# A two-layer spectral metaformer block: filter and weight set-up inside the ramp's ticks, and a finer order of the full tick

## The chip, the cores and the metric

One core of a Trainium2 chip runs the whole program. The metric is the device time of one execution in microseconds. The kernel before takes 5155.03 (median of 3 runs, 5151.31 to 5158.59).

A core has a matrix engine (TensorE, PE in the rows; PEld is its weight loading), VectorE (DVE), ScalarE (ACT), GpSimd (POOL) and SyncE (SP), which in this kernel issues all the transfers. Each works through its own list in order and waits on the others through semaphores.

## The reference

The input is 8 images of 128 x 128 pixels with 96 channels. Two layers follow each other, and each has two residual halves: a spectral convolution, and a small feed-forward net on every pixel. What one layer computes, cut to its core:

```python
z = (x - mean(x)) / sqrt(var(x) + 1e-6)                  # per pixel, over 96 channels
a = scale * relu(z @ w1.T)**2 + bias                     # 96 -> 192
F = rfft2(a)                                             # per channel, 128 x 65
r = softmax(soa(concat(mean(z), mean(relu(bn(z @ sp_w.T)))) @ fc1.T) @ fc2.T)
filt = [Rh @ cw @ Rw.T for cw in (cw0, cw1, cw2)]        # 16x9, 8x4, 24x13 -> 128 x 65
x = x + irfft2(F * sum(r[s] * filt[s])) @ w2.T           # 192 -> 96
z = (x - mean(x)) / sqrt(var(x) + 1e-5)
h = relu(q16(q8(z) @ q8(W1) + q8(b1)))                   # 96 -> 384; q8 is float8e5, q16 float16
x = x + q16(q8(h) @ q8(W2) + q8(b2))                     # 384 -> 96
```

The three filters of a layer are given small and are resized by two fixed matrices, Rh and Rw, before use. The filters do not depend on the image; the three weights r do.

## The kernel before

**Stages and groups.** Two layers of 8 images make 16 jobs, and each job is cut into 16 groups of 8 rows (or, in the middle stage, of 4 frequencies), so every stage has 256 groups. There are three stages, each a generator that yields between its steps:

- P (`pixels`): load x (step 0), statistics, scale on POOL (line 507), transpose on PE (`pt_a`), evict with ScalarE (`xT`), project in two halves (`pw0`, `pw1`, line 522), relu and square on ScalarE (`r`, `xs`), sum and difference of row pairs (`sd`, line 540), transform along the width (`pa0`, `pa1`, line 549), and store to memory (`a_d`, line 569).
- F (`frequencies`): load a_d and the half-resized filter `u_d` (tiles `al`, `ut`), weigh the filter on POOL (line 656), resize it along the height on PE (`pf`, line 668), transform along the height (`py`, line 702), multiply on VectorE (`pr`), add on POOL (`xf`), project to 96 channels (`pz`, lines 776 and 784), transform back (`pi`), and store (`y_d`). One group of 16 is "packed": it holds the two real frequencies, with an extra product `px`.
- S (`tokens`): load y_d and x, transform back along the width (`ps_r`), add, statistics and normalisation (`xn_c`), transpose (`pt_c`), and the feed-forward net in three blocks (`pm0` to `pm2`, evicted as `y16`, then `a16` and a cast to float8 `h`), second product (`po`), eviction (`o16`), bias (line 905), final addition on POOL and store (line 908).

N is the shared normalisation arithmetic of a tick; G is an image's gate (the softmax r).

**Ticks.** The program is a loop over ticks t from -4 to 299. F runs 19 groups behind P and S 40 behind. In each tick a written list gives the order of the steps: an entry ("S", 21, -2) gives step 21 of S to the group two behind. There are five lists: RAMP (t below 15, P alone), RISE (t = 15 to 37, P and F), TICK (t = 38 to 257, all three), FALL (258 to 275, F and S) and TAIL (S alone). The order of issue on each engine is the order of the list, since the kernel is written under a manual schedule:

```python
for place, (stage, step, ahead) in enumerate(order):
    for gate_step, image in gates.get(place, ()):
        advance("G", gate_step, image)
    i = t - offset[stage] + ahead
    advance(stage, step, i if stage == "N" else min(i, n - 1))
```

**Banks.** PSUM is cut into four double banks. `BANKS` (one table for each list) says which of the four a tile uses. A group of matmuls can start when the last reader of the tile before it in that bank is done, so a list and its bank table together decide where TensorE waits.

**Set-up.** Before the loop, `prepare` loads and prepares the weights of both layers, `load_filters` loads their filters, and `small_filters` resizes them along the width: for each layer 12 blocks of four products (line 284, 8 matmul instructions), two copies on ScalarE (298), two on VectorE (296), and a store to `u_d` (300). All of it stands ahead of the first x load in every engine's list, SP's included. Line numbers are those of the kernel before.

Of the kernel before, what the change touches and what calls it, by code (L numbers as in the profile page):

```python
# [10 lines left out]
F32 = mybir.dt.float32  # L11
F16 = mybir.dt.float16
# [28 lines left out]
UN = 8  # L41
NA, NY = 3, 3
LAG = 3
WE = M + SC
# [3 lines left out]
NORM_ACT, NORM_ACT_TAIL = (4, 5, 6, 7), (0, 1, 3, 4, 5, 7)  # L48
CAST_ACT, CAST_ACT_TAIL = (0, 1, 2), ()
SD_POOL_RAMP = ((0, 1), (1, 1))  # L50
# [3 lines left out]
    ("S", 4, 0), ("S", 21, -2), ("P", 10, -1), ("P", 11, -1), ("P", 0, 4), ("F", 2, 1),  # L54
    ("F", 3, 1), ("P", 2, 1), ("P", 1, 2), ("S", 5, 0), ("F", 4, 1), ("P", 12, -1),
    ("S", 6, 0), ("S", 22, -2), ("S", 1, 1), ("F", 5, 1), ("S", 7, 0), ("S", 14, -1),
    ("S", 2, 1), ("F", 9, 0), ("P", 3, 1), ("S", 8, 0), ("P", 13, -1), ("S", 15, -1),
    ("P", 14, -1), ("S", 16, -1), ("N", 0, 0), ("S", 17, -1), ("P", 4, 1), ("S", 9, 0),
    ("F", 6, 1), ("P", 5, 0), ("N", 1, 0), ("F", 10, 0), ("P", 15, -1), ("F", 11, 0),
    ("P", 6, 0), ("N", 2, 0), ("F", 7, 1), ("P", 16, -1), ("P", 17, -1), ("P", 18, -1),  # L60
    ("S", 10, 0), ("F", 12, 0), ("S", 0, 3), ("P", 19, -1), ("F", 13, 0), ("S", 11, 0),
    ("S", 18, -1), ("P", 7, 0), ("F", 8, 1), ("F", 14, 0), ("S", 12, 0), ("P", 8, 0),
    ("F", 0, 3), ("F", 1, 2), ("F", 15, 0), ("S", 19, -1), ("S", 13, 0), ("S", 3, 1),
    ("S", 20, -1), ("P", 9, 0),
# [3 lines left out]
    1: ((26, 0), (44, 1), (52, 2), (53, 3), (55, 4), (59, 5), (61, 6)),  # L68
    2: ((23, 7), (35, 8), (41, 9), (48, 10)),
# [3 lines left out]
    ("P", 1, 2), ("F", 3, 1), ("N", 0, 0), ("F", 4, 1), ("P", 3, 1), ("P", 5, 0),  # L73
    ("F", 10, 0), ("P", 14, -1), ("P", 15, -1), ("P", 0, 3), ("P", 4, 1), ("P", 6, 0),
    ("F", 5, 1), ("F", 11, 0), ("N", 1, 0), ("P", 16, -1), ("P", 17, -1), ("P", 7, 0),
    ("P", 8, 0), ("F", 6, 1), ("F", 7, 1), ("F", 1, 2), ("P", 18, -1), ("P", 19, -1),
    ("F", 12, 0), ("F", 8, 1), ("P", 9, 0), ("N", 2, 0), ("P", 10, 0), ("P", 2, 2),
    ("P", 11, 0), ("F", 13, 0), ("F", 14, 0), ("F", 0, 3), ("P", 12, 0), ("F", 2, 2),
    ("F", 15, 0), ("P", 13, 0), ("F", 9, 1),
)  # L80

# [924 lines left out]
```

## Time and profile before

| what | us |
|---|---|
| median of 3 runs | 5155.03 |
| the profiled execution, and its span | 5158.86, 5156.8 |
| first load of x issued | 109.75 |
| POOL scaling (L507) of the 1st, 4th and 18th group starts | 118.5, 138.1, 234.1 |
| its pace: ramp, rise, full ticks | 6.9, 14.3, 18.6 (most) |
| final addition (L908) in the fall and the tail, pace | 14.1, 8.8 |
| POOL idle until the bias (L905) before L908 | 1032.4 in 220 waits |
| mean granted TensorE clock | 0.983 |

The profile is of one execution. A row of instructions gives start and duration in us, then engine, line, operation, the tile written and the tiles read, the shape and a count; in brackets the idle time of the engine before it and what ended it. A row of a group gives a total in us, the mean of one in ns, and the idle time before. A row by stretch gives the busy time of each engine in a window with the number of its instructions. In a chain where every group starts as the last one lets it, the difference of two starts is what the first group costs; its own duration is some 0.2 longer, since matmuls overlap at their ends.

### The profile page before, as it was taken

The page shows a single profiled execution, that of the slowest core. Times are in us where ns is not written, and L with a number is a line of the kernel's source. Part 1 is how long each engine was busy: PE and PEld are TensorE (multiplying, and loading weights), DVE is VectorE, ACT ScalarE, POOL GpSimd, SP SyncE. Part 2 cuts the span into 40 slices and gives each one's busy share as a digit, 9 for nine tenths or more (in the row PEclk, how much of TensorE's full clock was granted, in tenths as well). Part 3 has the DMA queues.
Part 4 walks back from the last instruction along what each step waited for, and adds up shares of the span by engine and source line. Part 5 has one row for each costly group of instructions (what it writes and reads, how often), then busy time and mean ns, then how long its engine had stood idle before and what let it go on. Part 6 is the DMA issues. An engine that isn't in the chain of part 4 may idle for free. (4 is left out here: it accounts for less than half of the span.)

```text
span 5156.8 us, 123945 instructions
## 1 busy us (share of the span) xinstructions
PE 4888.7 (95%) x44232; PEld 3746.4 (73%) x44232; DVE 4532.4 (88%) x13904; ACT 4359.2 (85%) x7108; POOL 2608.7 (51%) x1947
## 2 busy tenths in 40 slices
PE   4899999999999999999999999999999999999976
PEld 1688777777777777777777777777777777777743
DVE  3888899898999999898998989989999989987888
ACT  2755689889888989889899888999888998987877
POOL 0655545545545545545455455555455554554457
PEclk9999999999999999999999999999999999999986
DMA  6466777777777777777777777777777777776753
GB/s 150 157 195 185 210 202 211 207 207 210 206 207 204 209 211 208 206 204 208 208 211 207 204 207 204 213 206 209 205 206 208 210 210 201 209 197 161 190 141 114
DMA packets 917034, 1020.95 MB, mean 198 GB/s; under 512 B 75826, under 2 KB 848914, under 8 KB 916082
## 3 DMA queue, kind: packets, MB, share of 16 engines
q1 hardware_dynamic: 916420, 1013.04, 70.2%
q8 instruction: 352, 5.77, 0.5%
q14 instruction: 262, 2.15, 0.1%
HBM read 598.92 MB, written 413.84 MB: 196 GB/s over the span
## 5 line engine op out<-in xcount | busy, mean ns | idle before, releaser
L908 POOL TENSOR_TENSOR y<-xr,o 128x768 f32<-128x768 f32 x256 | 421.8, 1648 | 1102.6 <-DVE o L905 1032.4
L522 PE MATMUL pw<-w,xT 97*128 97x240 f32 x4096 | 957.6, 377 | 4.2 <-DVE pr L730 2.1
L745 POOL TENSOR_TENSOR xf<-pr 128x768 f32<-128x768 f32 x512 | 931.6, 1821 | 38.3 <-DVE pr L730 26.1
L522 PEld LDWEIGHTS pw<-w,xT 97*128 97x128 f32 x4096 | 740.7, 191 | 150.0 <-ACT y L879 96.2
L879 ACT CAST y<-pm 128x1024 f16<-128x1024 f32 x768 | 771.7, 1008 | 54.4 <-PE pm L876 25.3
L702 PE MATMUL py<-k_fwd,al 128*128 128x128 f32 (+1 forms) x6208 | 806.2, 281 | 6.4 <-DVE pr L730 5.3
L534 POOL TENSOR_TENSOR acc<-acc,r 128x192 f32<-128x192 f32 x496 | 296.6, 598 | 987.3 <-ACT r L525 928.1
L726 DVE TENSOR_TENSOR pr<-py,cf 128x768 f32<-128x768 f32 x512 | 489.8, 957 | 332.3 <-PE py L702 311.9
L886 ACT ACTIVATE h<-a 128x1024 fp8e5<-128x1024 f16 x706 | 756.8, 1072 | 2.4 <-DVE a L882 2.4
L702 PEld LDWEIGHTS py<-k_fwd,al 128*128 128x128 f32 (+1 forms) x6208 | 727.5, 191 | 39.7 <-PE pt_c L866 6.9
L876 PE MATMUL pm<-xq,f_q 96*128 96x512 fp8e5 x1536 | 472.4, 390 | 103.8 <-ACT xq L869 82.6
L525 ACT ACTIVATE r<-pw 128x960 f32<-128x960 f32 x512 | 489.3, 956 | 94.7 <-PE pw L522 94.4
L656 POOL TENSOR_TENSOR ut<-ut,rw 112x768 f32<-112x768 f32 (+1 forms) x256 | 474.1, 1852 | 82.2 <-ACT rw L630 43.9
L540 DVE TENSOR_TENSOR sd<-xs 128x384 f32<-128x384 f32 x993 | 508.9, 552 | 4.2 <-ACT xs L528 3.5
L507 POOL TENSOR_TENSOR xn_a<-xt,n_rs 128x768 f32<-128x768 f32 x256 | 376.8, 1472 | 183.6 <-DMA xt<-in_x_dram 114.6
L528 ACT ACTIVATE xs<-r 128x768 f32<-128x768 f32 x512 | 438.0, 859 | 0.1
L852 ACT ACTIVATE xn_c<-xr,n_nb,n_rs 128x96 fp8e5<-128x96 f32 x1061 | 407.9, 459 | 31.8 <-DVE n_nb L473 31.8
L668 PEld LDWEIGHTS pf<-k_rh,ut 48*128 48x128 f32 x6080 | 361.7, 188 | 86.2 <-issue 78.5
L668 PE MATMUL pf<-k_rh,ut 48*128 48x128 f32 x6080 | 413.5, 282 | 5.0 <-POOL ut L656 1.8
L784 PE MATMUL pz<-w2a,xf 128*128 128x96 f32 x2048 | 418.1, 286 | 0.0
L784 PEld LDWEIGHTS pz<-w2a,xf 128*128 128x128 f32 x2048 | 312.1, 192 | 144.3 <-issue 142.8
L549 PE MATMUL pa<-sd,dft 64*64 64x384 f32 x4096 | 392.5, 496 | 7.1 <-ACT xT L514 4.5
(131 smaller groups left out, 10038.3 us busy)
## 6 DMA issues: line engine op xcount, KB each, us to landing
a_d<-at SPq DMA_DIRECT2D x256, 768.0 KB
al<-a_d SPq DMA_DIRECT2D x1024, 192.0 KB
y_d<-yt SPq DMA_DIRECT2D x512, 192.0 KB
v<-y_d SPq DMA_DIRECT2D x256, 384.0 KB
ut<-u_d SPq DMA_DIRECT2D x256, 336.0 KB
xt<-in_x_dram SPq DMA_DIRECT2D x512, 96.0 KB
xr<-in_x_dram SPq DMA_DIRECT2D x256, 192.0 KB
mid<-y SPq DMA_DIRECT2D x256, 192.0 KB
```

Source lines behind the costliest of these rows:

```text
L522: mm(o, xT[:, 4 * a + 2 * i + j, :], wt["w1"], start=True, stop=True)
L525: nc.scalar.activation(r.rearrange("p a s c -> p a (s c)"), pw, AF.Relu)
L540: on.tensor_tensor(sd[:, e], xs[:, 0], xs[:, 1], op)
L656: nc.gpsimd.tensor_tensor(ut[:, -n:], ut[:, -n:], _bc_mid(jb.rw, n), ALU.mult)
L668: mm(pf[:, i, t * 128 : (t + 1) * 128], utf[64 * i : 64 * i + NHS, c0 : c0 + 128], kt["rh"][64 * i : 64 * i + NHS, :], start=True, stop=True,)
L702: mm(py[p0:p1, t, e, :], alf[:, e, c0 + p0 : c0 + p1], f, start=True, stop=True)
L726: nc.vector.tensor_tensor(p0, yv, crb, ALU.mult)
L745: nc.gpsimd.tensor_tensor(xf.rearrange("p t e f -> p (t e) f"), pr[:, 0].rearrange("p t r k -> p t (r k)"), pr[:, 1].rearrange("p t r k -> ...
L784: mm(pz[:, t, j, e, :], xf[:, 2 * t, e, :], wt["w2c" if t else "w2a"], start=False, stop=j == e == 1,)
L876: mm(pm[:, s, :], fk, xq[:, s, :], start=True, stop=True)
L879: nc.scalar.copy(y16, pm)
L886: nc.scalar.activation(hk, a16, AF.Copy, saturate=False)
```

## The change

**Set-up.** The block before the loop is gone. The first x load and the projection weights of layer 0 (`projection_weights`) come first. Everything else becomes an event, issued after step 9 of P in a given tick: filters and the width matrix at t = 0, other weights at 2, constants at 4 and 6, filter padding at 13, filters of layer 1 at 15, feed-forward weights at 17 and 23, projection and other weights of layer 1 at 19 and 21, its padding at 34. The filter blocks become a stage U of three steps (products; ScalarE copies; VectorE copies and store), one block per tick: layer 0 in t = 1 to 12 of the ramp, layer 1 in t = 22 to 33 of the rise. The temporary pool `us` lives until t = 36, with single buffers (three for a block's result), and then gives its space to the tiles of S.

**Steps.** `pa0` and `pa1`, `pf0`, `pf1` and `px`, `cf0` and `cf1`, and the addition and the statistics of S each become steps of their own. The later steps count up: S ends with step 23, F with 18, P with 20.

**Orders.** All five lists and bank tables are new. In TICK the products now follow each other so (bank in brackets): px (2, packed group only), py0 (2), pt_c (1), pz first part (3), pm2 (0), pm0 (1), pz second part (3), pt_a (0), pw0 (3), pa0 (1), pa1 (0), po (2), py1 (3), pi (1), pm1 (2), pw1 (0), ps_r (3), pf0 (1), pf1 (0). Before: pf, py0, pt_c, ps_r, pm0, pt_a, pm2, pw, pz first part, pa, pz second part, py1, pi, pm1, po, pw. The addition and store of S (step 23) comes two ticks behind the bias (step 22); before, the two (22, 21) stood in one tick.

**Engines.** In the ramp one of the two differences that POOL made goes to VectorE. In the tail the eviction `o16` goes from ScalarE to VectorE, the bias from POOL to VectorE, and one of the three float8 casts from POOL to ScalarE; the set of normalised rows on ScalarE stays six of eight.

```diff
+NU = NG // UN
+UPAUSE, UEND = 21, 36
+EVENTS_AFTER = ("P", 9)
...
-NORM_ACT, NORM_ACT_TAIL = (4, 5, 6, 7), (0, 1, 3, 4, 5, 7)
-CAST_ACT, CAST_ACT_TAIL = (0, 1, 2), ()
-SD_POOL_RAMP = ((0, 1), (1, 1))
+NORM_ACT, NORM_ACT_TAIL = (4, 5, 6, 7), (1, 3, 4, 5, 6, 7)
+CAST_ACT, CAST_ACT_TAIL = (0, 1, 2), (0,)
+SD_POOL_RAMP = ((0, 1),)
 TICK = (
-    ("S", 4, 0), ("S", 21, -2), ("P", 10, -1), ("P", 11, -1), ("P", 0, 4), ("F", 2, 1),
-    ("F", 3, 1), ("P", 2, 1), ("P", 1, 2), ("S", 5, 0), ("F", 4, 1), ("P", 12, -1),
-    ("S", 6, 0), ("S", 22, -2), ("S", 1, 1), ("F", 5, 1), ("S", 7, 0), ("S", 14, -1),
-    ("S", 2, 1), ("F", 9, 0), ("P", 3, 1), ("S", 8, 0), ("P", 13, -1), ("S", 15, -1),
-    ("P", 14, -1), ("S", 16, -1), ("N", 0, 0), ("S", 17, -1), ("P", 4, 1), ("S", 9, 0),
-    ("F", 6, 1), ("P", 5, 0), ("N", 1, 0), ("F", 10, 0), ("P", 15, -1), ("F", 11, 0),
-    ("P", 6, 0), ("N", 2, 0), ("F", 7, 1), ("P", 16, -1), ("P", 17, -1), ("P", 18, -1),
-    ("S", 10, 0), ("F", 12, 0), ("S", 0, 3), ("P", 19, -1), ("F", 13, 0), ("S", 11, 0),
-    ("S", 18, -1), ("P", 7, 0), ("F", 8, 1), ("F", 14, 0), ("S", 12, 0), ("P", 8, 0),
-    ("F", 0, 3), ("F", 1, 2), ("F", 15, 0), ("S", 19, -1), ("S", 13, 0), ("S", 3, 1),
-    ("S", 20, -1), ("P", 9, 0),
+    ("F", 4, 1), ("S", 2, 1), ("S", 23, -3), ("F", 5, 1), ("P", 11, -1), ("P", 12, -1),
+    ("P", 13, -1), ("S", 6, 0), ("F", 6, 1), ("F", 12, 0), ("F", 7, 1), ("P", 0, 3),
+    ("F", 13, 0), ("F", 8, 1), ("S", 15, -1), ("S", 16, -1), ("P", 2, 1), ("S", 7, 0),
+    ("S", 8, 0), ("F", 14, 0), ("P", 3, 1), ("S", 17, -1), ("S", 9, 0), ("S", 3, 1),
+    ("P", 5, 0), ("P", 1, 2), ("F", 9, 1), ("F", 15, 0), ("P", 14, -1), ("N", 0, 0),
+    ("P", 4, 1), ("S", 18, -1), ("N", 1, 0), ("N", 2, 0), ("S", 4, 1), ("P", 15, -1),
+    ("P", 16, -1), ("S", 19, -1), ("S", 20, -1), ("P", 6, 0), ("F", 10, 1), ("F", 16, 0),
+    ("P", 17, -1), ("S", 10, 0), ("P", 18, -1), ("P", 19, -1), ("P", 7, 0), ("S", 21, -1),
+    ("S", 11, 0), ("P", 20, -1), ("F", 17, 0), ("P", 8, 0), ("F", 0, 3), ("F", 11, 1),
+    ("F", 18, 0), ("F", 1, 2), ("S", 0, 3), ("P", 9, 0), ("S", 12, 0), ("P", 10, 0),
+    ("S", 1, 2), ("F", 2, 2), ("S", 5, 1), ("S", 13, 0), ("F", 3, 2), ("S", 14, 0),
+    ("S", 22, -1),
 )
 
 GATE = {
-    1: ((26, 0), (44, 1), (52, 2), (53, 3), (55, 4), (59, 5), (61, 6)),
-    2: ((23, 7), (35, 8), (41, 9), (48, 10)),
+    1: ((10, 0), (15, 1), (17, 2), (21, 3), (30, 4), (31, 5), (42, 6)),
+    2: ((2, 7), (4, 8), (22, 9), (31, 10)),
 }
...
 RAMP = (
-    ("P", 17, -1), ("N", 1, -1), ("P", 2, 2), ("P", 0, 4), ("P", 3, 2), ("P", 18, -1),
-    ("P", 19, -1), ("P", 6, 1), ("P", 12, 0), ("P", 7, 1), ("P", 4, 2), ("P", 1, 4),
-    ("N", 2, -1), ("P", 8, 1), ("P", 13, 0), ("P", 14, 0), ("N", 0, 0), ("P", 9, 1),
-    ("P", 10, 1), ("P", 15, 0), ("P", 11, 1), ("P", 16, 0), ("P", 5, 2),
+    ("U", 0, 0), ("P", 19, -1), ("P", 0, 4), ("P", 11, 0), ("N", 1, -1), ("P", 6, 1),
+    ("U", 1, 0), ("P", 12, 0), ("P", 3, 2), ("P", 20, -1), ("P", 1, 4), ("U", 2, 0),
+    ("P", 4, 2), ("P", 7, 1), ("P", 8, 1), ("P", 13, 0), ("P", 14, 0), ("N", 0, 0),
+    ("N", 2, -1), ("P", 2, 3), ("P", 9, 1), ("P", 10, 1), ("P", 15, 0), ("P", 16, 0),
+    ("P", 17, 0), ("P", 5, 2), ("P", 18, 0),
 )
...
 BANKS = {
-    "ps_g": 0, "ph": 1, "pl": 3, "pa0": 2, "pa1": 3, "pw0": 1, "pw1": 1, "pt_a": 3,
-    "pf0": 3, "pf1": 2, "py0": 0, "py1": 1, "pz": 0, "pi": 2, "ps_r": 2, "pt_c": 1,
-    "pm0": 1, "pm1": 3, "pm2": 0, "po": 0, "px": 1, "pg": 0,
+    "ps_g": 1, "ph": 1, "pl": 2, "pa0": 1, "pa1": 0, "pw0": 3, "pw1": 0, "pt_a": 0,
+    "pf0": 1, "pf1": 0, "py0": 2, "py1": 3, "pz": 3, "pi": 1, "ps_r": 3, "pt_c": 1,
+    "pm0": 1, "pm1": 2, "pm2": 0, "po": 2, "px": 2, "pg": 2,
 }
...
+    def filters(i):
+
+        l, n0 = i // NU, i % NU * UN
+        pss = []
+        for i in range(2):
+            pss.append(bank2(f"ps_u{i}")[:NKW, :, : UN * UM])
+        for i in range(M // UM):
+            mm(
+                pss[i // 2][:, i % 2, :].rearrange("p (n m) -> p n m", m=UM),
+                kt["rw"][32 * i : 32 * i + NWS],
+                cws[l][32 * i : 32 * i + NWS, :, n0 : n0 + UN].rearrange("p m n -> p n m"),
+                start=True,
+                stop=True,
+            )
+        yield
+        u = us.tile([NKW, UN, M], F32, name="u", bufs=3)
+        uv = u.rearrange("p n (i a m) -> p i a n m", a=2, m=UM)
+        for i, ps in enumerate(pss):
+            for a in range(2):
+                o = ps[:, a, :].rearrange("p (n m) -> p n m", m=UM)
+                if i:
+                    nc.vector.tensor_copy(uv[:, i, a], o)
+                else:
+                    nc.scalar.copy(uv[:, i, a], o)
+            if i:
+                n1 = n0 if n0 < NHS else 64 + n0 - NHS
+                nc.sync.dma_start(u_d[l][:, n1 : n1 + UN, :], u)
+            yield
+
+    def padding(l):
+
+        dst = u_d[l][:, NHS:64, :].rearrange("k (a n) m -> k a (n m)", n=4)
+        nc.sync.dma_start(dst, _bc_mid(pad, 4))
...
-        yield
+            yield
...
-        pf0, pf1 = filter_mm(0), filter_mm(2)
+        pf0 = filter_mm(0)
+        yield
+        pf1 = filter_mm(2)
+        yield
         px = filter_mm_packed() if packed else None
         yield
         py0 = fft_mm(0)
         yield
-        cf0, cf1 = filter_out(pf0, px), filter_out(pf1)
+        cf0 = filter_out(pf0, px)
+        yield
+        cf1 = filter_out(pf1)
...
         for a, op in enumerate((ALU.add, ALU.subtract)):
             nc.vector.tensor_tensor(xv[:, a], xv[:, a], pr[:, 1], op)
+        yield
         x8 = xr.rearrange("p s h c -> p (s h) c")
         nm = norms[-1].stats(1, x8)
...
-        o16 = ab.tile([128, RG, C], F16, name="o16")
-        nc.scalar.copy(o16.rearrange("p (a b) c -> p a (b c)", a=2), po[:, :, : RH * C])
-        yield
-        on = nc.gpsimd if on_pool["b2"] else nc.vector
-        on.tensor_tensor(o16, o16, _bc_mid(wt["b2"], RG), ALU.add)
-        yield
-        y = ab.tile([128, 2, RH, C], F32, name="y")
+        o16 = pools[0].tile([128, RG, C], F16, name="o16")
+        ov, pv = o16.rearrange("p (a b) c -> p a (b c)", a=2), po[:, :, : RH * C]
+        if on_act["out"]:
+            nc.scalar.copy(ov, pv)
+        else:
+            nc.vector.tensor_copy(ov, pv)
+        yield
+        nc.vector.tensor_tensor(o16, o16, _bc_mid(wt["b2"], RG), ALU.add)
...
+    events = {
+        0: (lambda: load_filters(0, layers[0]), lambda: constants("rw")),
+        2: (lambda: other_weights(0, layers[0]),),
+        4: (lambda: constants("fwd", "inv", "rh"),),
+        6: (lambda: constants("fwd0", "inv0", "rh0"),),
+        13: (lambda: padding(0),),
+        15: (lambda: load_filters(1, layers[1]),),
+        17: (lambda: constants("idft"), lambda: token_weights(0, layers[0])),
+        19: (lambda: projection_weights(1, layers[1]),),
+        21: (lambda: other_weights(1, layers[1]),),
+        23: (lambda: token_weights(1, layers[1]),),
+        34: (lambda: padding(1),),
+    }
+
+    def group(i):
+
+        i -= 1
+        return min(i, NU - 1) if i < UPAUSE else min(i - UPAUSE + NU, 2 * NU - 1)
...
-    on_act.update(norm=NORM_ACT, cast=CAST_ACT)
-    on_pool.update(sd=SD_POOL_RAMP, b2=False)
+    on_act.update(norm=NORM_ACT, cast=CAST_ACT, out=True)
+    on_pool.update(sd=SD_POOL_RAMP)
...
+    offset["N"], offset["U"] = -first, 0
     with tc.manual_schedule():
-        for t in range(-first, n + offset["S"] + last + 1):
+        advance("P", 0, 0)
+        projection_weights(0, layers[0])
+        for t in range(-first, n + offset["S"] + behind + 1):
...
-                on_act.update(norm=NORM_ACT_TAIL, cast=CAST_ACT_TAIL)
-                on_pool.update(b2=True)
+                on_act.update(norm=NORM_ACT_TAIL, cast=CAST_ACT_TAIL, out=False)
             banks.update(places)
+            if t == UEND:
+                early.close()
+                pools.append(ctx.enter_context(tc.tile_pool(name="sb", bufs=2)))
...
-                advance(stage, step, i if stage == "N" else min(i, n - 1))
+                last = i if stage == "N" else group(i) if stage == "U" else min(i, n - 1)
+                advance(stage, step, last)
+                if (stage, step) == EVENTS_AFTER:
+                    for event in events.get(t, ()):
+                        event()
```

## The prediction

> **What bounds the kernel now.** I read the busy shares first, then the same shares by stretch, then the TensorE rows of one tick in order of time, then the waits.
>
> ```profile
> PE 4888.7 (95%) x44232; PEld 3746.4 (73%) x44232; DVE 4532.4 (88%) x13904; ACT 4359.2 (85%) x7108; POOL 2608.7 (51%) x1947
> ```
>
> By stretch (columns: PE, PEld, DVE, ACT, POOL busy, granted clock, DMA share, GB/s): set-up, ramp, rise, full ticks, tail. The sixth line is the POOL scaling L507, once per tick, in the full ticks.
>
> ```profile
> 0.00:109.70 109.70, 50.27 (x200) 15.31 (x200) 35.70 (x99) 24.00 (x59) 3.31 (x7) 1.00 0.65 158
> 151.00:172.00 21.00, 18.54 (x123) 13.00 (x124) 20.17 (x68) 16.91 (x32) 16.51 (x16) 1.00 0.50 171
> 290.00:545.00 255.00, 252.96 (x2195) 210.09 (x2190) 217.62 (x571) 147.41 (x267) 140.25 (x107) 1.00 0.65 186
> 1000.00:4000.00 3000.00, 2941.23 (x27285) 2286.36 (x27278) 2711.66 (x8411) 2700.62 (x4334) 1522.79 (x1132) 1.00 0.74 207
> 4960.00:5135.00 175.00, 126.55 (x909) 66.60 (x908) 164.96 (x486) 137.75 (x257) 123.91 (x96) 0.70 0.42 124
> 1000.00:4000.00 3000.00, 234.12 (x159) 1.00 0.74 207
> ```
>
> To be seen: 110 us of set-up in which no engine is half busy; a ramp at 96% of VectorE (20.17 of 21.00) and 6.86 us a tick; then TensorE at 98-99% in rise and full ticks; a tail on VectorE. 3000/159 is 18.9 us a full tick, of which there are 220 (t = 38 to 257); most are 18.64, and those with a gate or the packed chunk bring the mean up.
>
> TensorE in one such tick (start, us of a row, line, tile):
>
> ```profile
> 2000.48 1.60 PE L702 MATMUL py<-k_fwd,al 128*128 128x128 f32 x12
> 2001.92 0.61 PE L866 MATMUL pt_c<-ident,xn_c 128*96 128x128 fp8e5 x8
> 2002.46 0.88 PE L832 MATMUL ps_r<-v,k_idft 64*64 64x384 f32 x8
> 2003.64 0.59 PE L876 MATMUL pm<-xq,f_q 96*128 96x512 fp8e5 x2 [0.30 <-ACT xq L869]
> 2004.07 1.04 PE L511 MATMUL pt_a<-ident,xn_a 128*96 128x128 f32 x8
> 2004.95 0.60 PE L876 MATMUL pm<-xq,f_q 96*128 96x512 fp8e5 x2
> 2005.49 1.89 PE L522 MATMUL pw<-w,xT 97*128 97x240 f32 x8
> 2007.31 1.14 PE L776 MATMUL pz<-w2b,xf 64*128 64x96 f32 x16
> ...
> 2017.58 1.61 PE L668 MATMUL pf<-k_rh,ut 48*128 48x128 f32 x24
> 2019.12 0.38 PE L702 MATMUL py<-k_fwd,al 128*128 128x128 f32 x1
> ```
>
> From py to py is 18.64, and each row starts about when the last lets it: the tick is one chain of 16 groups. The waits of 1000-4000 us name what is not work in it:
>
> ```profile
> PEld pw L522 <- ACT y L879: 70.2, 159, 0.4
> PE pm L876 <- ACT xq L869: 55.6, 159, 0.8
> ```
>
> ps_r to pm takes 1.18 there and 0.81 at best elsewhere, so xq costs 0.37 a tick; pm to pw takes 0.54 against 0.43 for pm to pt_a, so y costs 0.11. Work without waits is 18.64 - 0.48 = 18.16. That is all a new order can take out of a common tick: 0.48 x 220 = 106 us.
>
> [...]
>
> **Set-up into the ramp.** Now the first x load is issued at 109.75 and the ramp's steady pace holds from the fourth scaling (138.07) to the eighteenth (234.1): 14 ticks. Afterwards the x load is first on SP, at about 0.8; the same run-in of 28.3 brings the fourth scaling to 29. Layer 0's projection is ready at 14.25 now, the first pw comes 13.4 after the first x load, so they nearly meet; its ten VectorE operations (0.2 each) stand ahead of the first statistics: 3 us. So 32.
>
> Twelve ramp ticks then carry a filter block. Rows of now: 8 matmuls 1.73, two VectorE copies of 0.55 done in 1.02, two ScalarE copies 0.85, one 390 KB store with 1.8 us of SP issue. VectorE has 6.59 a tick now (20.17 x 6.86/21); 1.02 more, and 0.55 for the half difference that comes back from POOL (1.38 there), make 8.2. TensorE makes 6.06 + 1.73 = 7.8, ScalarE 6.4. SP's own issue is 3.5 (four x loads 3.11, one store 0.35), with the block 5.3; it is covered. I take 8.3 a tick: 12 x 8.3 + 2 x 6.86 = 113. The constants at t = 4 and 6 are loads alone (0.3 to 0.7 of SP issue each). The weights at t = 2 and the first block, which waits for filter loads that took 7 to 15 us to land in the set-up and are issued about a tick ahead: 5. The eighteenth scaling falls at 150 instead of 234: 84 gained. Ends: 7.8 a tick and no wait gives 90; 9.4 (everything of a block in series: 6.86 + 1.73 + 0.85) and 13 of waits gives 62.
>
> The rise has no such room: at 99% of TensorE, 12 blocks of 1.73 cost 20.8 in full. Four weight events stand there too; each loads on SP and then has VectorE, once TensorE, wait for it (bva landed 2.9 after its issue). If SP runs ahead they cost 6 in all, if each load lands late 4 each. VectorE's 2 us of slack per rise tick covers their small operations. So 27, between 21 and 40. **Net: 57, between 22 and 69.**
>
> **The order of the full tick.** The same instructions, so the same kinds of group: py 1.44, pt_c 0.54, pz(b) 1.07, pm2 0.43, pm0 0.43, pz(a) 1.86, pt_a 0.87, pw0 1.81, pa 1.45, po 1.02, py 1.37, pi 1.29, pm1 0.43, pw1 1.82, ps_r 0.81, pf 1.54: 18.18, each the start-to-start of the same kind of neighbours now. What matters is whether a bank is free in time. With py at 0:
> - xq now has pz(b) and pm2 between pt_c and pm0. On ScalarE the run is xs (0.85, from r at 17.7), cf0 and cf1 (0.69 each), a cast (0.96), xq (0.92); each is its row's duration less the 0.1 by which the next overlaps it. It ends at 21.8, or 3.3 of the next tick; pm0 is due at 3.48. The 0.37 goes.
> - pw1 has bank 0, freed by VectorE long before. The 0.11 goes.
> - pw0 has bank 3 after pz: zt cannot start before 5.94 (last pz row plus 0.28) and takes 0.87. Only pt_a stands between; pw0 waits 0.26. New.
> - pf1 has bank 0 after pw1, so it needs r(pw1). Before r, ScalarE has yo (pi done, 14.0; 0.43), four xn (0.36 each), y16 of pm1 (0.91) and r (0.95 in full): 17.7. pf1 is due 0.1 earlier. New.
> - The rest is early: py1 by 0.7 (r of pw0), pi by 0.6, pm1 by over 1.
>
> So 18.18 + 0.36 = 18.54, 0.10 under now: **22 us gained**. All waits gone would be 101 gained; each of the three close places late by 0.3 more would be 0.8 a tick, 176 lost. POOL's final addition moves two ticks behind its VectorE input; POOL idles 1032 us for that input now, and it is off the path: no gain by itself. SP's load into the fifth xr buffer now waits for it; it ends about 14.4, ahead of yt's store (15.3) in the same queue: nothing. Splitting py, cf and pa into steps issues nothing new. Ticks with gate or packed chunk, rise and fall (41 ticks) get new orders too: nothing, give or take 15.
>
> **The tail.** 20 ticks of 8.86 on VectorE, whose tiny operations there are stretched beside POOL's casts. The same operation in the tail, and in the full ticks:
>
> ```profile
> L468 DVE SCALAR_TENSOR_TENSOR n_a<-n_rs 128x8 f32<-128x8 f32 x10 | 10.0, 999 | 0.0
> L468 DVE SCALAR_TENSOR_TENSOR n_a<-n_rs 128x16 f32<-128x16 f32 x159 | 26.7, 168 | 0.0
> ```
>
> With L469 (946 against 193) and two xn_c (703 against 323) that is 2.3 a tick. One cast of three leaves POOL, which may give back a third, 0.8; VectorE takes the eviction of po (nearest row L841, 0.95) and the bias (0.55). ScalarE changes 0.8 for 1.07. Between 1.0 gained (no stretch left) and 0.7 lost a tick; I take 0. Ends: 20 gained, 14 lost.
>
> [...]
>
> **Sum.** 57 + 22 = 79 off the profiled execution's 5158.9 is 5079.9; that execution stands 3.8 above the median of the runs, so 5076.
>
> **The rivals.**
> 1. *No waits in the full tick* (18.2-18.3): the margins at zt and r are a tenth or two, and back-to-back ScalarE rows overlap by 0.1. 5158.9 - 57 - 85 - 3.8 = 5013. Against: zt can't begin before pz ends.
> 2. *The set-up is hidden only half*: blocks and weights hold the in-order queues in ramp and rise; set-up gain 22, tick gain 22: 5111. For it: u waited on its own stores 75 us in the set-up; against: the stores go two every 4.5 us now (24 from 54.7 to 109), then one every 8.3.
> 3. *Slower*: ScalarE's run yo, xn, y16, r before pf1 in bank 0. 57/220 is 0.26, so it decides where pf1 waits 0.36 beyond the walk (tick 18.90). At 0.5 beyond, the ticks lose 88 against now, less 57: 5158.9 + 31 - 3.8 = 5186. For it: ScalarE has 17.0 busy (2700.6/159) of 18.5, one run without a gap from pi to pm0; against: the 0.6 idle before zt takes up a slip each tick.
> 4. *The move doesn't happen*: the x load still waits behind weights. No row for it: SP's list starts with x.
>
> **How the numbers follow.** Forecast 0.55 (5040 to 5105), rival 1 0.2, rival 2 0.12, rival 3 0.13. No change within 0.2% (10 us, about what a measurement here can tell) lies between rivals 2 and 3: 0.04, taken from both. Faster 0.84, same 0.04, slower 0.12. The range leaves out the lower fifth of rival 1 and most of rival 3: 4990 to 5150.
>
> **What would show it.** The first L507 at about 12 us (8.7 after the first x load, as now, and 3) and the eighteenth near 150; ramp ticks near 8.3; rise ticks with a block 1.7 longer; L507 18.5 apart in the full ticks; pm no longer waiting for xq, pw for zt instead; n_a of the tail under 999. It is wrong if L507 is over 18.9 apart, or if pf waits for r in every tick.

## The result and the profile after

The changed kernel takes 5155.97 us (median, 5151.33 to 5163.92) beside 5153.16 of the kernel before in the same session: ratio 1.0005, interval 0.9996 to 1.0014. That is no change, where the forecast had 5076. The profiled execution of after took 5153.64, with a span of 5151.7 (before: 5158.86 and 5156.8).

The lines of after that answer those of before. First the busy shares of the page, then busy time by stretch in the columns of before: the full ticks, then the last ticks. The third fence line is the POOL scaling, now L518, alone in the same 3000 us.

```profile
PE 4931.3 (96%) x44232; PEld 3767.3 (73%) x44232; DVE 4596.3 (89%) x13962; ACT 4385.9 (85%) x7108; POOL 2582.1 (50%) x1889
...
1000.00:4000.00 3000.00, 2965.70 (x27330) 2302.74 (x27330) 2752.47 (x8426) 2719.68 (x4342) 1563.44 (x1133) 1.00 0.71 208
...
1000.00:4000.00 3000.00, 233.79 (x159) 1.00 0.71 208
```

The busy shares are those of before within a point or two, and the 3000 us hold 159 scalings, as they did. A sum over the whole span hides what moved, so here is the start of chosen POOL scalings (before L507, after L518) and final additions (L908, L930), read from the two traces as stages:

| stage, from ... to | before, us | after, us | change | forecast |
|---|---|---|---|---|
| start to the 1st scaling | 118.5 | 16.3 | -102.2 | |
| ramp: to the 18th scaling | 115.6 | 145.3 | +29.7 | the two together -84 |
| rise: to the 40th scaling | 312.3 | 388.4 | +76.1 | +27 |
| entry into the full ticks: to the 46th scaling | 105.3 | 128.7 | +23.4 | 0 |
| full ticks: to the 251st scaling | 3874.3 | 3869.3 | -5.0 | -22 |
| the rest: fall and tail | 630.8 | 603.7 | -27.1 | 0 |
| span | 5156.8 | 5151.7 | -5.1 | -79 |

So the 110 us of set-up did leave the front, and it came back in the ramp and above all in the rise. The rise of after, by busy time in windows (columns as above):

```profile
162.00:240.00 78.00, 50.05 (x301) 37.58 (x300) 42.20 (x124) 27.80 (x50) 22.00 (x19) 0.70 0.63 161
240.00:360.00 120.00, 103.79 (x790) 79.91 (x790) 90.15 (x217) 55.04 (x102) 49.22 (x37) 0.90 0.52 145
360.00:550.00 190.00, 188.41 (x1584) 147.02 (x1583) 178.86 (x415) 108.01 (x202) 94.65 (x75) 1.00 0.67 191
```

In the rise of before TensorE was at 80% for the first 26 us and at 98 to 99% from there on. Now it is at 64% of the first 78 us and 86% of the next 120, and the granted clock falls with it, to 0.70 and 0.90; only from 360 is the stage whole again. What it waits for stands in the rows of the timeline (start, duration, in brackets the idle time before and what ended it): first VectorE, then TensorE, then SyncE, whose rows (SPq) are the issues of transfers.

```profile
200.25 0.58 DVE L398 CAST f_q<-f_f 96x384 fp8e5<-96x384 f32 x2 [16.66 <-DMA f_f<-in_L_ffn_W_dram]
235.66 0.19 DVE L345 TENSOR_SCALAR bva<-bva 97x48 f32<-97x48 f32 x1 [7.93 <-DMA bva<-in_L_conv_bn_var_dram]
278.86 0.15 DVE L384 TENSOR_SCALAR dc<-dc 64x1 f32<-64x1 f32 x1 [7.90 <-DMA dc<-in_L_conv_soa_bias_dram]
323.28 0.36 DVE L398 CAST f_q<-f_f 96x384 fp8e5<-96x384 f32 x1 [8.78 <-DMA f_f<-in_L_ffn_W_dram]
```

```profile
238.20 1.08 PE L358 MATMUL ps_w<-raw,cen 96*96 96x240 f32 x2 [12.33 <-DVE cen L355]
239.73 3.57 PE L533 MATMUL pw<-w,xT 97*128 97x240 f32 x8 [0.44 <-ACT w L360]
277.89 0.51 PE L372 MATMUL ps_w<-fc1g,cen 96*96 96x36 f32 x2 [7.32 <-DMA fc1g<-in_L_conv_fc_dram]
326.98 2.93 PE L713 MATMUL py<-k_fwd,al 128*128 128x128 f32 x12 [8.43 <-DVE pr L741]
```

```profile
190.39 3.28 SPq L661 DMA_DIRECT2D al<-a_d  x4
193.72 0.60 SPq L663 DMA_DIRECT2D ut<-u_d  x1
194.37 0.48 SPq L264 DMA_DIRECT2D k_idft<-in_c_idft_dram  x1
194.89 0.90 SPq L320 DMA_DIRECT2D f_f<-in_L_ffn_W_dram  x2
```

Every weight event issues its loads and, in the same tick, the VectorE or TensorE instruction that needs them. VectorE reaches that instruction at once and stands: 16.66 us on f_f, which SyncE issued only at 194.89, since its own list had an image load and two groups of F's loads (`al`, `ut`) first. Of VectorE's four waits above, 3.4 to 11.3 us pass before SyncE comes to the issue, and 2.2 to 5.3 from the issue to the landing. Behind the waiting cast stand the statistics and the products of the ticks, so TensorE stands too, and the matmuls after the wait run slowly: 12 of py take 2.93 us at 326.98, behind 8.43 us of idling, and 1.60 in the full ticks, and 8 of pw 3.57 at 239.73, 1.5 us behind 12.33 of idling, and 1.89 in the full ticks. The granted clock is 0.50 from 326.9 to 330 and from 240 to 243.3, and 1.00 again from 334 to 340 and from 250 to 256. That the idling lowers the clock is my reading of these rows; no run isolates it.

The full tick of after, one TensorE stretch of the timeline in order of time (start, duration, line, tile):

```profile
2005.08 1.04 PE L522 MATMUL pt_a<-ident,xn_a 128*96 128x128 f32 x8
2006.20 1.89 PE L533 MATMUL pw<-w,xT 97*128 97x240 f32 x8
...
2013.19 0.60 PE L895 MATMUL pm<-xq,f_q 96*128 96x512 fp8e5 x2
2013.63 1.78 PE L533 MATMUL pw<-w,xT 97*128 97x240 f32 x8
2015.35 0.88 PE L850 MATMUL ps_r<-v,k_idft 64*64 64x384 f32 x8
2016.15 1.92 PE L679 MATMUL pf<-k_rh,ut 48*128 48x128 f32 x24
2018.00 1.60 PE L713 MATMUL py<-k_fwd,al 128*128 128x128 f32 x12
```

ScalarE in the same tick:

```profile
2015.21 0.99 ACT L898 CAST y<-pm 128x1024 f16<-128x1024 f32 x1
2016.11 0.97 ACT L536 ACTIVATE r<-pw 128x960 f32<-128x960 f32 x1
```

And the waits of 1000 to 4000 us in after (total, times, longest), which replace those of xq and y:

```profile
PEld pw L533 <- ACT zt L807: 45.7, 139, 0.3
PEld pf L679 <- ACT r L536: 39.7, 159, 0.5
```

The waits for xq and y are gone as forecast, pt_a to pw0 takes 1.12 instead of 0.87 (pw0 waits for zt), and pf takes 1.85 instead of 1.54: its second half, due 0.77 after the start of pf at 2016.92, waits for r, which ends at 2017.08, and so in each of the 159 ticks. The median tick is 18.60 us, 0.04 under before.

In the last ticks, n_a stands at 406 ns where it stood at 999, and the final additions come every 8.03 us, where they came every 8.85:

```profile
4993.80:5122.40 128.60, 101.51 (x739) 50.13 (x736) 124.21 (x433) 115.27 (x209) 62.01 (x50) 0.80 0.49 145
...
L479 DVE SCALAR_TENSOR_TENSOR n_a<-n_rs 128x8 f32<-128x8 f32 x12 | 4.9, 406 | 0.0
```

### The profile page after: what moved, and what is told of

The parts are those of the page before. It is cut to its first block, busy times and chain, and to the rows that moved or that the text cites. A ratio compares the mean times of both kernels' runs of the same rounds, so it can differ in the third digit from the quotient of the medians.

```text
span 5151.7 us, 123630 instructions
## 1 busy us (share of the span) xinstructions
PE 4931.3 (96%) x44232; PEld 3767.3 (73%) x44232; DVE 4596.3 (89%) x13962; ACT 4385.9 (85%) x7108; POOL 2582.1 (50%) x1889
## 5 line engine op out<-in xcount | busy, mean ns | idle before, releaser
L545 POOL TENSOR_TENSOR acc<-acc,r 128x192 f32<-128x192 f32 x496 | 340.2, 686 | 1727.9 <-ACT r L536 1042.2
L533 PEld LDWEIGHTS pw<-w,xT 97*128 97x128 f32 x4096 | 764.9, 192 | 153.9 <-ACT zt L807 63.9
L898 ACT CAST y<-pm 128x1024 f16<-128x1024 f32 x768 | 748.3, 1006 | 147.2 <-PE pm L895 147.1
L713 PE MATMUL py<-k_fwd,al 128*128 128x128 f32 (+1 forms) x6208 | 821.7, 284 | 23.0 <-ACT cf L724 10.1
L905 ACT ACTIVATE h<-a 128x1024 fp8e5<-128x1024 f16 x726 | 772.3, 1064 | 11.4 <-DVE a L901 11.3
L679 PEld LDWEIGHTS pf<-k_rh,ut 48*128 48x128 f32 x6080 | 378.6, 188 | 207.8 <-issue 139.6
L679 PE MATMUL pf<-k_rh,ut 48*128 48x128 f32 x6080 | 469.3, 289 | 21.5 <-POOL ut L667 8.0
L518 POOL TENSOR_TENSOR xn_a<-xt,n_rs 128x768 f32<-128x768 f32 x256 | 379.8, 1484 | 186.9 <-DVE n_rs L481 158.9
L930 POOL TENSOR_TENSOR y<-xr,o 128x768 f32<-128x768 f32 x256 | 421.3, 1646 | 87.7 <-ACT cf L720 44.7
L895 PE MATMUL pm<-xq,f_q 96*128 96x512 fp8e5 x1536 | 434.7, 389 | 20.6 <-ACT y L898 9.8
L901 DVE TENSOR_SCALAR a<-y,b 128x1024 f16<-128x1024 f16 x768 | 371.5, 486 | 73.5 <-ACT y L898 66.2
L912 PEld LDWEIGHTS <-h 128*128 128x128 fp8e5 x6144 | 285.3, 100 | 158.4 <-issue 127.7
```

Source lines behind the costliest of these rows:

```text
L533: mm(o, xT[:, 4 * a + 2 * i + j, :], wt["w1"], start=True, stop=True)
L679: mm(pf[:, i, t * 128 : (t + 1) * 128], utf[64 * i : 64 * i + NHS, c0 : c0 + 128], kt["rh"][64 * i : 64 * i + NHS, :], start=True, stop=True,)
L713: mm(py[p0:p1, t, e, :], alf[:, e, c0 + p0 : c0 + p1], f, start=True, stop=True)
L895: mm(pm[:, s, :], fk, xq[:, s, :], start=True, stop=True)
L898: nc.scalar.copy(y16, pm)
L905: nc.scalar.activation(hk, a16, AF.Copy, saturate=False)
```

## The experiments

All ratios are against the kernel before, run on the same chip beside them; after itself stands at 1.0005. "Rise" is the time from the 18th to the 40th scaling, "entry" from the 40th to the 46th, "tick" the mean of the 205 full ticks behind it.

**Weight loads ahead of their use, in lumps.** The loads of an event go into an earlier tick, its arithmetic stays where it was.

```diff
+        -3: (lambda: other_loads(0, L0),),
...
+        5: (lambda: constants("idft"), lambda: token_loads(0, L0)),
...
+        7: (lambda: projection_loads(1, L1),),
+        9: (lambda: other_loads(1, L1),),
+        11: (lambda: token_loads(1, L1),),
...
-        17: (lambda: constants("idft"), lambda: token_weights(0, layers[0])),
...
+        17: (lambda: token_weights(0, L0),),
```

> The changed kernel, with every weight load of the events issued 5 to 14 ticks before its first use (in the ramp, t = -3 to 11), into tiles of its own; the uses stay in their ticks. Theory 1 (the rise loses its time where VectorE and TensorE stand in order behind weight loads that SP issues late, and the granted clock falls in those waits): the start of group 39's scaling comes from 550 to about 500, the clock between 162 and 360 us rises from 0.70-0.90 to over 0.95, the ramp's 12 us hole at t = 2 closes, and the whole falls by 50 to 65, to 5090-5105. Theory 2 (the rise's new order and the filter blocks themselves cost it): less than 15 is gained, and the rise ticks after t = 17 stay over 17 us.

5137.85 us, ratio 0.9968 (0.9954 to 0.9982). The rise went from 388.4 to 351.1, but the 18th scaling came at 177.4 instead of 161.6: the lumps of weight loads now stood ahead of the image loads in SyncE's queue, and the ramp lost 16 of the 37 us. The whole gained 18 us on after where 50 to 65 were expected.

**The token stage's first loads one or two ticks earlier.** TensorE's first ps_r of after waits for its load, since the entry tick issues the load and, with the new order, the product for the same group:

```profile
575.10 1.56 PE L850 MATMUL ps_r<-v,k_idft 64*64 64x384 f32 x8 [9.31 <-DMA v<-y_d]
```

```diff
     ("P", 2, 2), ("F", 4, 2), ("F", 5, 2), ("P", 12, 0),
+    ("S", 0, 4),
 )
```

> The changed kernel, with the first loads of the token stage (step 0 of S) two ticks earlier, at the end of the rise's list. Theory 1 (at the first full tick the product ps_r stands right behind its own load and TensorE idles 9 us, then runs at a lower clock): 10 to 20 less, 5136-5146, ps_r no longer waits for v. Theory 2 (the entry costs what it costs because the full tick's order starts with empty pipelines): within 5 of the changed kernel.

5145.28 us, ratio 0.9982 (0.9972 to 0.9991). The entry went from 128.7 to 119.2. The 9.5 us are the wait in the row above, which is gone; 14 of the 23 lost at the entry stay.

**The old order and banks of the full tick, in the new step numbers.**

```diff
 TICK = (
-    ("F", 4, 1), ("S", 2, 1), ("S", 23, -3), ("F", 5, 1), ("P", 11, -1), ("P", 12, -1),
...
+    ("S", 5, 0), ("S", 22, -2), ("P", 10, -1), ("P", 11, -1), ("P", 0, 4), ("F", 2, 1),
...
-    "ps_g": 1, "ph": 1, "pl": 2, "pa0": 1, "pa1": 0, "pw0": 3, "pw1": 0, "pt_a": 0,
+    "ps_g": 0, "ph": 1, "pl": 3, "pa0": 2, "pa1": 3, "pw0": 1, "pw1": 1, "pt_a": 3,
```

> The changed kernel with the full tick's order, gate places and banks of before, in the new step numbers; rise, ramp, fall and tail stay new. Theory 1 (the new order is worth next to nothing: the waits for zt and r take the place of those for xq and y16): the scalings stay 18.6 apart in the full ticks, 5140-5160 in all, less whatever the entry into the full ticks gives back (up to 20, since ps_r comes a tick later there). Theory 2 (my walk, 0.10 a tick): 22 more than the changed kernel, about 5178.

5133.93 us, ratio 0.9959 (0.9945 to 0.9974): faster than after. The tick is 18.898 against 18.875, so the new order is worth 0.023 x 205 = 5 us; the entry is 106.6 against 128.7, so it costs 22 there. The loss at the entry therefore belongs to the order and banks of the full tick, and not to the rise ahead of it. In the new order S takes two of its early steps a tick sooner; how that makes the loss is shown for the 9.5 us of the run before alone. On the whole the new order lost.

**Block 4 of the normalisation from ScalarE to VectorE.**

```diff
-NORM_ACT, NORM_ACT_TAIL = (4, 5, 6, 7), (1, 3, 4, 5, 6, 7)
+NORM_ACT, NORM_ACT_TAIL = (5, 6, 7), (1, 3, 4, 5, 6, 7)
```

> The changed kernel with one of four normalised rows moved from ScalarE to VectorE in the full ticks (0.36 off ScalarE's run yo, xn, y16, r; 0.24 more on VectorE). Theory 1 (pf1 waits 0.30 a tick for r(pw1) behind that run): the wait goes, the pace falls from 18.6 to 18.3-18.4, and 45 to 65 are gained (5090-5110). Theory 2 (the pw0 wait for zt or VectorE takes it over at once): less than 15.

5125.71 us, ratio 0.9942 (0.9928 to 0.9957). The tick fell to 18.561, 0.31 less: pf is back at 1.54, so the wait for r was a wait for ScalarE's list to reach r. But the same setting holds in the fall, and there it cost 39 us, which the expectation had left out. The fall (219th to 232nd final addition) by busy time, this kernel first, then after:

```profile
4706.70:4928.20 221.50, 187.06 (x1683) 145.64 (x1681) 172.83 (x485) 150.58 (x239) 89.67 (x54) 0.91 0.60 155
```

```profile
4773.00:4955.40 182.40, 171.06 (x1685) 129.43 (x1684) 158.41 (x472) 155.10 (x252) 90.07 (x54) 1.00 0.74 189
```

In the fall the transpose pt_c waits for VectorE's part of the normalisation, in this kernel (first two lines) far more than in after (third):

```profile
PEld L885 <- DVE xn_c L877: 26.3, 14, 2.0
PE pt_c L885 <- DVE xn_c L877: 23.8, 13, 1.9
```

```profile
PEld L885 <- DVE xn_c L877: 0.6, 1, 0.6
```

**The old engines in the last ticks.** The new order and banks of the tail stay.

```diff
-NORM_ACT, NORM_ACT_TAIL = (4, 5, 6, 7), (1, 3, 4, 5, 6, 7)
-CAST_ACT, CAST_ACT_TAIL = (0, 1, 2), (0,)
+NORM_ACT, NORM_ACT_TAIL = (4, 5, 6, 7), (0, 1, 3, 4, 5, 7)
+CAST_ACT, CAST_ACT_TAIL = (0, 1, 2), ()
...
-                on_act.update(norm=NORM_ACT_TAIL, cast=CAST_ACT_TAIL, out=False)
+                on_act.update(norm=NORM_ACT_TAIL, cast=CAST_ACT_TAIL, out=True)
+                on_pool.update(b2=True)
```

> The kernel after, with the engines of the last ticks as before the change: normalisations of blocks 0, 1, 3, 4, 5 and 7 on ScalarE, all casts on GpSimd, the bias addition on GpSimd, the copy out of the accumulator on ScalarE; order and banks of the last ticks stay those of after. The profiles of before and after show 141.6 and 128.6 us from the 236th to the 252nd final addition. Theory (the assignment is what made the last ticks shorter): this stretch goes back to about 140, and the whole comes to about 5168 us, ratio 1.0027 of before. Rival (the new order and banks of the last ticks made them shorter, and the engines are indifferent, as the forecast had it): the stretch stays within 2 us of 128.6, ratio 1.0005.

5190.02 us, ratio 1.0066 (1.0049 to 1.0083). The stretch is 149.7 us (140 expected), longer than with after's engines (128.6) and longer than before (141.6): the change of engines is worth 21 in this stretch, more than its whole gain of 13, and the new order with the old engines is 8 worse than the old order.

**One of these engines alone: the third cast back to GpSimd.**

```diff
-CAST_ACT, CAST_ACT_TAIL = (0, 1, 2), (0,)
+CAST_ACT, CAST_ACT_TAIL = (0, 1, 2), ()
```

> The kernel after, with one edit: in the last ticks the casts of the third that ScalarE took go back to GpSimd, which then has all three a tick, as before the change; normalisations, bias addition and copy out stay those of after. Theory A (the forecast's reading: GpSimd's casts stretch VectorE's small operations, and VectorE, 97% busy in the last ticks of after, sets their length): n_a goes from 406 ns back towards 999, and the stretch from the 236th to the 252nd final addition grows from 128.6 us by 5 to 15. Theory B (ScalarE, 90% busy, sets their length): it shrinks by up to 10 us as 1.04 us a tick leave ScalarE. Theory C (neither; it is the order and the chain through the last product): within 3 us of 128.6.

5169.31 us, ratio 1.0028 (1.0017 to 1.0038). The stretch is 138.3, 9.7 more, as theory A had it, but for another reason: n_a did not go back towards 999, it fell. What TensorE waits for is the last cast itself. A group and one wait of this kernel on TensorE's two rows, 5040 to 5140 us, and the same wait in after, 5010 to 5110:

```profile
L479 DVE SCALAR_TENSOR_TENSOR n_a<-n_rs 128x8 f32<-128x8 f32 x12 | 3.0, 253 | 4.2 <-ACT n_rs L476 4.2
```

```profile
PEld L912 <- POOL h L907: 15.0, 11, 1.4
PE po L912 <- POOL h L907: 13.1, 11, 1.3
```

```profile
PEld L912 <- POOL h L907: 1.3, 8, 0.2
```

The second product of a group needs all three casts, and GpSimd takes 1.04 us for each; in after the whole idle time ahead of po and its weight loads is 1.7 us in a stretch of the same length. So in this order a cast on ScalarE gains by lying beside the other two. Theory A's price was right and its mechanism wrong. This cast is 9.7 of the 21 us that the engines are worth; the other edits were not run one by one.

**Weight loads spread over the ticks.** As in the first experiment, but two or three transfers a tick, over the ticks -3 to 16, and the zeroing of the second gate matrices ahead of the loop.

```diff
+    queue = [
+        *fc_loads(0, L0),
+        *(lambda k=k: constants(k) for k in ("fwd", "inv", "rh", "fwd0", "inv0", "rh0")),
+        *other_loads(0, L0), lambda: constants("idft"), *token_loads(0, L0),
+        *projection_loads(1, L1), *fc_loads(1, L1), *other_loads(1, L1), *token_loads(1, L1),
+    ]
+    places_of = [t for t in range(-3, 17) if t != 0 for _ in range(2 if t < 3 else 3)]
+    for t, go in zip(places_of, queue):
+        events[t] = events.get(t, ()) + (go,)
```

> The kernel after, with the weight loads of the ticks (not the arithmetic on them) moved ahead and spread, two or three transfers a tick, on SyncE's queue, over the ticks from -3 to 16, so that no tick has a lump of them; the loads ahead of the loop stay as they are, but for the zeroing of the two second gate matrices, which comes to stand there. Theory (the rise was lost to in-order waits behind late weight loads, and the earlier run that moved them lost in the ramp because lumps of them stood ahead of the image loads): the 18th scaling of the input within 5 us of after's 161.6, from there to the 40th scaling about 350 us against 388, whole about 5120 us, ratio 0.993. Rival A (the early transfers delay the image loads even spread out): the 18th scaling near 177, ratio near 0.996 as with lumps. Rival B (the zeroing costs what it saved): the first scaling some us after 16.3 and nothing else changes in size.

5133.39 us, ratio 0.9956 (0.9941 to 0.9971). The rise is 351.1 again. The 18th scaling is at 170.1: half of the lumps' loss is gone and half is not, so neither the theory nor rival A got its number. The rise by windows now:

```profile
170.00:215.00 45.00, 33.71 (x200) 26.37 (x199) 26.64 (x88) 20.19 (x36) 14.49 (x14) 0.74 0.72 184
215.00:341.00 126.00, 120.05 (x972) 91.91 (x976) 114.99 (x277) 69.34 (x131) 62.54 (x50) 0.97 0.64 180
```

With the loads there in time, TensorE is at 95% from 215 on and the clock at 0.97: the idling and the low clock went together.

**Banks of the full tick.** Two edits there: block 4 to VectorE in the full ticks alone, and the tiles of banks 2 and 3 in two sets that swap the two banks from tick to tick, so that pw0 takes a bank that VectorE frees (py0 had it before) and not the one zt reads.

```diff
+NORM_ACT_TICK = (5, 6, 7)
...
-    2: ((2, 7), (4, 8), (22, 9), (31, 10)),
+    2: ((2, 7), (4, 8), (22, 9), (23, 10)),
...
+ODD = ("py0", "pw0", "py1", "ps_r", "px", "pg")
+EVEN = ("pz", "po", "pm1", "pl")
...
+            if order is TICK:
+                banks.update({k: 2 + t % 2 for k in ODD})
+                banks.update({k: 3 - t % 2 for k in EVEN})
```

> The kernel after, with two edits in the full ticks alone: block 4 of the normalisation goes from ScalarE to VectorE (the rise and the fall keep after's split), and the accumulators of two of the four banks swap from tick to tick, so that the projection's first group no longer takes the bank that the copy of the mixer's result (zt) holds, with one gate step moved ahead. Measured before: block 4's move alone shortened the full tick from 18.875 to 18.561 us but lengthened the fall by 39 us. Theory (ScalarE's queue sets the full tick through the releases of the banks: 0.24 us of zt wait and up to 0.30 us of r wait a tick): tick of 18.0 to 18.3, fall back at about 182 us from the 219th to the 232nd final addition, whole about 5035 us, ratio 0.977. Rival (the waits are only handed on to the next late release): tick 18.5, whole about 5090 us, ratio 0.9875.

5024.81 us, ratio 0.9747 (0.9733 to 0.9762). The tick is 18.271 (median 17.95), the fall 182.7 us, as in after. The same TensorE rows in this kernel:

```profile
2015.23 1.04 PE L525 MATMUL pt_a<-ident,xn_a 128*96 128x128 f32 x8
2016.10 1.79 PE L536 MATMUL pw<-w,xT 97*128 97x240 f32 x8
```

```profile
2008.01 1.61 PE L682 MATMUL pf<-k_rh,ut 48*128 48x128 f32 x24
2009.54 1.60 PE L716 MATMUL py<-k_fwd,al 128*128 128x128 f32 x12
```

pt_a to pw0 is 0.87 and pf to py 1.53: both waits are gone, and nothing took their place.

**The banks alone.** The swap and the gate step, with the normalisation as in after.

> The kernel after, with the two banks swapped from tick to tick in the full ticks and the one gate step moved, but the normalisation's split between ScalarE and VectorE left as it is. Measured so far: 18.875 us a full tick in after, 18.561 with the normalisation's edit, 18.271 with both. Theory (the waits for zt and r are waits for a bank and nothing else): the tick falls by about 0.29 to 0.54 us, to 18.3 to 18.6, whole 5045 to 5095 us, ratio 0.979 to 0.988. Rival (ScalarE's queue is the bound in after; a freed bank only lets TensorE come sooner to the next release of ScalarE): the tick falls by less than 0.1 us, whole 5135 us or more, ratio above 0.996.

5093.10 us, ratio 0.9879 (0.9863 to 0.9896). The tick is 18.586, 0.29 less than after; pt_a to pw0 is 0.87, and pf still waits for r:

```profile
PEld pf L681 <- ACT r L538: 40.5, 162, 0.5
```

So the two waits are independent: 0.29 for the bank, 0.31 for ScalarE's list, and 0.60 together (18.875 - 18.271). Each wait also lengthened the group that had waited: pw0 takes 1.82 in after and 1.72 here, the second half of pf 0.87 in after and 0.77 without the wait (medians).

**Three edits together.** The spread loads, the earlier first step of S, and both edits of the full tick.

> Three edits to the kernel after together: the weight loads spread over the early ticks on SyncE's queue, the token stage's first step appended to the rise (it alone gave 10 us at the entry into the full ticks), and the two edits in the full ticks (block 4 of the normalisation on VectorE, two banks swapped from tick to tick). If the losses are in separate stages, as the table by stages has it, the gains add: 36 in ramp and rise, 10 at the entry, 65 to 120 in the full ticks: 4990 to 5045 us, ratio 0.968 to 0.979. If the stages hand their loss on (a shorter rise only meets a longer entry), the whole is less than the sum of the runs of the single edits by over 15 us.

4986.62 us, ratio 0.9671 (0.9657 to 0.9686). The edits alone gained 22.6, 10.7 and 131.2 from after's 5155.97, 164.4 in sum; together they gain 169.4. The losses lay in separate stages.

**The weight loads on ScalarE's queue.** As the last, with the loads of the early ticks issued by ScalarE.

```diff
-        nc.sync.dma_start(temps[l][name], view)
+        eng[0].dma_start(temps[l][name], view)
...
+        eng[0] = nc.scalar
```

> The kernel of the run before with its three edits together, but the spread weight loads and the constants of the early ticks are issued by ScalarE on its own queue instead of by SyncE. In that run the 18th scaling of the input still began 8 to 9 us later than in after (169 against 161.6), and VectorE waited for the image loads more (24.7 us against 12.6 between 60 and 165 us). Theory (the image loads stand behind the weight loads in SyncE's queue): the 18th scaling near 160, waits for the image loads back to about 12 us, whole about 4978 us, ratio 0.9655. Rival (the transfers share the DMA engines, whichever queue issues them, and ScalarE's own issue time comes on top): the 18th scaling at 169 or later, whole 4986 us or more.

4969.55 us, ratio 0.9640 (0.9626 to 0.9655), the fastest of all. The 18th scaling is at 152.0, against 169.2 with the same loads on SyncE, and the rise stays at 351.3. (The 24.7 us that the expectation names were measured with the loads spread and nothing else.) Waits of VectorE for the image loads from 60 to 165 us, first with the three edits on SyncE's queue, then here:

```profile
DVE st L467 <- DMA xt<-in_x_dram: 26.7, 12, 3.8
```

```profile
DVE st L467 <- DMA xt<-in_x_dram: 11.9, 11, 2.4
```

The same bytes move in the same ticks; only the queue differs. What the ramp lost to weight loads it lost in SyncE's list.

## Why the prediction was wrong

**Set-up: net 57 forecast, 4 lost.** Up to the 40th scaling after is 3.6 us later than before (550.0 against 546.4). Two terms failed.

- *The ramp gain of 84.* The first scaling came at 16.3 (12 forecast), the 18th at 161.6 (150 forecast). The common ramp tick with a block, 6.6 to 9.2 us, lies about the 8.3 of the walk. The "5" for the weights at t = 2 and the first block is the term that was too small: the tick of that event took 20.3 us, 12 more than the walk's 8.3, and SyncE stood 7.8 of it until VectorE had zeroed a matrix that a load fills. Measured gain 72.5, inside the ends of 62 to 90 (by its own terms the upper end is 95: 6 for the ticks and 5 for the waits on top of 84).
- *The rise loss of 27.* "If SP runs ahead they cost 6 in all, if each load lands late 4 each" is the step that failed. The blocks were sized well: rise ticks with one take 16.1 to 16.3 us, those without 14.3, so 1.8 each against 1.73, and 12 make 22. But the four weight events of the rise (t = 17, 19, 21 and 23) cost 37 together, some 9 each, which is what moving their loads gave in four runs. I priced a load's latency, 2.9 us from issue to landing (2.2 to 5.3 here), and not the time that SyncE needs to come to the issue, another 3.4 to 11.3. What idles is then not one engine but the lists behind it, and the clock falls (0.70 from 162 to 240). The last 17 of the 76 us stay open. Some 8 of them lie in the first three ticks of the rise, where the clock is 0.74 even with the loads in time. There SyncE's first load of F waits for a store of a_d, 4.9 us in before and 9.6 in after, and 2.4 more there for the filter loads of layer 1, which the event at t = 15 puts there; no run moved those.

**Rival 2** named this mechanism ("blocks and weights hold the in-order queues in ramp and rise") and left the set-up a gain of 22 where 4 were lost. Its 22 is the lower end of my own range, in which a late load costs 4.

**The full tick: 22 forecast, 5 gained.** The forecast's reading of the tick held step by step: xq and y16 went, pw0 waits for zt 0.25 (0.26 forecast), pf1 waits for r. Only the last was mis-sized, 0.31 against 0.10, and not on ScalarE's side: in the median tick r ends 17.67 after py0, as the walk had it (17.7). TensorE comes to pf1 earlier than walked, at 17.52 instead of 17.6, starts it at 17.73, and pf1 then takes 0.10 longer. The median tick is 18.60 instead of 18.54. The sign "it is wrong if pf waits for r in every tick" came true. Rival 3 was the same wait; it would have decided from 0.36 beyond the walk, and it came 0.2 beyond. The 18.16 that I took for the work without waits was 0.2 too much: with both waits gone the median tick is 17.95, each group on the heels of the last.

**Entry: 0 forecast ("new orders too: nothing, give or take 15"), 23 lost.** The new order of the tick does two early steps of S a tick sooner, so the first full tick needs data at once that is only then loaded; 9.5 of it is the wait for v, and the other 14 are not traced to rows.

**Tail: 0 forecast (20 gained to 14 lost), 27 gained in fall and tail.** The engines were changed in the right direction; my reason was not the deciding one. I took the stretch of n_a for a cost of GpSimd's casts in proportion to their number. It did fall from 999 to 406 ns, but with all three casts on GpSimd it was 253. What the moved cast shortens in the order of after is the way to po. The 0 that I took between 1.0 gained and 0.7 lost a tick came out as 0.8 gained.

In sum, ramp, full ticks, fall and tail gained 72.5 + 5.0 + 27.1, and rise and entry took 76.1 + 23.4 of it. Of those 99.5 the loads moved ahead took back 37 and the earlier first step of S 9.5; the loads on ScalarE's queue also brought the 18th scaling from 161.6 to 152.0.

## What to carry to other kernels

The price of a load that was moved into the pipeline was its place in the issuing queue (3.4 to 11.3 us) on top of its latency (2.2 to 5.3): issue it some ticks ahead of its first reader (5 to 14 in the first run), move the load and the arithmetic apart, and try a queue whose owner has slack (ScalarE's brought the 18th scaling from 169.2 to 152.0). When an order leaves an engine waiting for a bank, look which reader frees it and how far down that reader's own list the reading stands; a second engine may free another bank earlier (0.29 us a tick here), or take a few instructions off the list (0.31). A setting that serves two stages with different bounds should be set for each: block 4 on VectorE gains 64 us in the full ticks and loses 39 in the fall.

## What the runs showed of the hardware

The small VectorE operation n_a, with two inputs in SBUF, did not slow down in proportion beside a GpSimd cast here; its row ends when that one's does. Between the 236th and the 252nd final addition of after all 16 n_a meet a cast and end 19 to 21 ns behind its end, and in before the 16 n_a and the next operation of this kind end 14 to 22 ns behind the two casts they meet. The timeline of before (start, duration):

```profile
5057.38 2.21 POOL L888 CAST h<-a 128x1024 fp8e5<-128x1024 f16 x2 [1.43 <-DVE a L882]
5057.62 1.00 DVE L468 SCALAR_TENSOR_TENSOR n_a<-n_rs 128x8 f32<-128x8 f32 x1
...
5058.65 0.95 DVE L469 TENSOR_TENSOR n_a<-n_a,n_v 128x8 f32<-128x8 f32 x1
5059.63 0.17 DVE L470 SCALAR_TENSOR_TENSOR n_rs<-n_a,n_rs 128x8 f32<-128x8 f32 x1
```

Two casts fill 5057.38 to 5059.59; the first n_a ends at 5058.62 and the second at 5059.60, and the third operation, with no cast beside it, takes 0.17. So 999 ns is the rest of a cast and not a rate, and where it falls is a question of order, which is why it didn't follow the number of casts: with three on GpSimd the mean of n_a is 999 ns in before, 601 in the run with the old engines and 253 in the one with the third cast back, and with two, in after, 406. In the full ticks of after (1000 to 4000 us) none of the 636 sd and of the 159 of each small operation of the normalisation, all with two SBUF inputs, lies beside a GpSimd instruction, while those with one input in PSUM do so at their usual duration (the larger pr, 957 ns beside, 297 of them, and 950 alone, 20).
